# A graph network's adjacency matrix for sorted edges: equal edges summed on VectorE, degrees behind the comparisons, all of it ahead of the branch

## The chip, the core and the metric

The kernel runs on one core of a Trainium2 chip. A core has TensorE (PE in the profile, with weight loads as PEld), VectorE (DVE), ScalarE (ACT), GpSimd (POOL) and SyncE (SP), which run side by side and wait for each other with semaphores. SP and ACT issue the plain DMAs, POOL the indirect ones (scatters and gathers by a list of row numbers). All DMAs share 16 DMA engines. The metric is the device time of one launch in microseconds (us).

## What is computed

A stack of four graph layers over 3125 nodes with 128 features and 50,000 edges, whose list is sorted by destination. Each layer has the form `x = layernorm(x + layer(x))`. The first and the last are chains of graph convolutions (3 and 10 of them); the two between work edge by edge (an attention and a gate). Of these, only what the first needs is touched by the change:

```python
def _gcn_layer(x, src, dst, ew, W, b):
    """PyG GCNConv: out = D^-1/2 (A + I) D^-1/2 (x W) + b."""
    n = x.shape[0]
    loop = jnp.arange(n)
    s = jnp.concatenate([src, loop])
    d = jnp.concatenate([dst, loop])
    w = jnp.concatenate([ew, jnp.ones((n,), ew.dtype)])
    deg = jax.ops.segment_sum(w, d, num_segments=n)
    dinv = jnp.where(deg > 0, jax.lax.rsqrt(deg), 0.0)
    norm = dinv[s] * w * dinv[d]
    h = x @ W
    out = jax.ops.segment_sum(h[s] * norm[:, None], d, num_segments=n)
    return out + b
```

## The kernel before

**The adjacency matrix.** A convolution is done as a dense product: the kernel writes A + I, 3200 x 3125 in float32, into DRAM, and each of the 13 convolutions streams it through PE (line 625, tile `acc`). The matrix lies in seven banks of 464 columns, numbered 0 to 6, in two DRAM tables: `adj0` (banks 0 to 3) and `adj4` (banks 4 to 6); the profile calls both `adj`. A convolution takes the banks from 6 down to 0, 50 matmuls each, in chunks that SP loads (`adj_k`; some chunks stay in SBUF). `Convolutions` also multiplies by the weights (`po`) one bank later.

**Filling it.** `fill` (105) makes a tile `eye` on POOL (a memset of 6320 elements and a copy of the identity) and has ACT issue one DMA of 5.8 MB per bank that writes the identity. Then the edges are added by POOL: 406 indirect scatters (517), each with 128 single values `total` to 128 addresses `at`. A scatter writes, it doesn't add. So edges with equal source and destination must first be summed into the first of them, and the later ones sent to spare rows ahead of the matrix.

**Sorted and unsorted edges.** `stretches` (221) loads the destinations as one run of 392 per partition (`run`: 127 rows in one DMA and the last row in another), tests that they are sorted and spread as expected, and leaves a flag. Every engine reads the flag and branches (1509 to 1511). The branch for sorted edges is the one that runs here; the other one builds the matrix by a general method (`build`, 270).

**Preparing sorted edges.** `SortedBuild` cuts the 28 stretches of 14 x 128 edges into five overlapping passes; each knows which banks its edges can fall into (first and last stretch, first and last bank, and the bank from which the banks are complete after it):

```python
PASSES = ((20, 28, 4, 7, 5), (16, 20, 4, 5, 4), (12, 17, 0, 4, 3), (3, 12, 0, 3, 1), (0, 3, 0, 1, 0))
```

Pass q is loaded as three windows (`src_w`, `dst_w`, `ew_w`) with C = 112, 56, 70, 126 or 42 edges per partition and W = 39 neighbours to the left, to the right or both. Where a window would reach past either end of the list (passes 0 and 4) it is loaded as 127 rows and one row. The method `prepare` (400) has an inner function of the same name (416). For a pass that does, all in order on DVE: a `key` per edge; `same`, 39 comparisons with the neighbours; `more`, the weights of the equal ones. PE then adds these up in `sum`: 39 float32 matmuls with the identity for the weights of later equal edges (two passes of PE each in the profile) and 39 bfloat16 ones to see whether an equal edge came before. DVE goes on with some 20 small operations on C elements (addresses, `lo` and `hi` of the destination). `degrees` (478) handles 14 columns of edges: DVE makes the one-hot tiles `ohl` (14 x 128) and `ohh` (14 x 25, times the weight), and 14 float32 matmuls add them into `deg_ps`. `settle` (463) reads `sum` and forms `total` and `at`. The order is written out by hand with `InOrder`: for each pass prepare, four groups of degrees, settle; then the rest of the 28 groups of degrees. Last come `deg`, a square root on ACT, and `dinv` (508). A pass's scatters are issued when the first convolution comes to a bank that needs them (510 to 525); that bank's loads wait for the pass's last eight scatters.

**Order around it.** `fill` for banks 6 to 4, the test, and the windows of pass 0 are ahead of the branch (1505 to 1508); `load_edges` (138) loads `dst_i`, `src_i`, `ew_c` and the features `x` on SP's and ACT's queues. Behind the branch are a second `eye` with the fills of banks 3 to 0, the other passes' windows, the five passes and the degrees, and then the first layer `l0` with its three convolutions. Its operands are `xs = x * dinv`, so it begins behind `dinv`. SP, ACT and POOL each work their instructions off in order. A DMA from SP or ACT reuses one of eight semaphores in turn, and waits until the earlier DMA on it has landed.

Of the kernel before, what the change touches and what calls it, by code (L numbers as in the profile page):

```python
# [9 lines left out]
F32 = mybir.dt.float32  # L10
I32 = mybir.dt.int32
# [37 lines left out]
def tile_gnn_stack(ctx: ExitStack, tc: tile.TileContext, a: dict, out: bass.AP):  # L49
# [55 lines left out]
    def fill(pool, banks):  # L105
        wide = NP - P + NBK * BW
        eye = pool.tile([P, wide], F32, name="eye")
        nc.gpsimd.memset(eye, 0.0)
        nc.gpsimd.tensor_copy(eye[:, NP - P:NP], ident)
        for b in banks:  # L110
            v = eye[:, b * BW:b * BW + BW]
            nc.scalar.dma_start(bank(b), bass.AP(tensor=v.tensor, offset=v.offset,
                                                 ap=[v.ap[0], [P, NT], [1, BW]]))
# [24 lines left out]
    def load_edges():  # L138
        nc.sync.dma_start(dst_i, a["dst_c"])
        nc.scalar.dma_start(src_i, a["src_c"])  # L140
        nc.sync.dma_start(ew_c, a["ew_c"])
        nc.vector.tensor_copy(dst_f, dst_i)
        nc.scalar.dma_start(x, a["x"].rearrange("(t p) d -> p t d", p=P))
# [126 lines left out]
    def build():  # L270
        with (
# [9 lines left out]
            fill(b1, reversed(range(HALF)))  # L281
# [81 lines left out]
    class SortedBuild:  # L363
# [5 lines left out]
        def __init__(self, early):  # L369
            self.at, self.total, self.ready, self.last = [], [], {}, []  # L370
            self.passes = list(enumerate(PASSES))
            self.st = [self.load(early, 0)]
# [27 lines left out]
        def prepare(self, pool, scratch, ps):  # L400
# [5 lines left out]
            ident_b = scratch.tile([P, P], BF16, name="ident_b")  # L406
            ve.tensor_copy(ident_b, ident)
            deg_ps = ps.tile([P, NT], F32, name="deg_ps")
# [7 lines left out]
            def prepare(q):  # L416
# [4 lines left out]
                both = ps.tile([P, 512], F32, name="both")  # L421
                ve.tensor_copy(both[:, :W + C], key[:, :W + C])
                ve.tensor_copy(both[:, 256:256 + C + W], t["ew"])
                same = scratch.tile([P, W, W + CM], BF16, name="same")[:, :, :W + C]
                ve.tensor_tensor(same, shifts(key, 1, W + C),
                                 both[:, None, :W + C].to_broadcast([P, W, W + C]), op=OP.is_equal)
                more = scratch.tile([P, W, CM], F32, name="more")[:, :, :C]
                ve.tensor_tensor(more, same[:, :, W:], shifts(both, 257, C), op=OP.mult)
                t["sum"] = ps.tile([P, 2, 256], F32, name="sum")
                for k in range(W):  # L430
                    pe_.matmul(t["sum"][:, 0, :C], ident, more[:, k, :], start=(k == 0), stop=(k == W - 1))
                for k in range(W):
                    pe_.matmul(t["sum"][:, 1, :C], ident_b, same[:, k, W - 1 - k:W - 1 - k + C],
                               start=(k == 0), stop=(k == W - 1))

                t["own"] = own = scratch.tile([P, C], F32, name=f"own{q}")
                ve.tensor_tensor(own, t["src"][:, mid], t["dst"][:, mid], op=OP.is_equal)
                ve.tensor_add(own, own, t["ew"][:, :C])
                dst = scratch.tile([P, C], F32, name=f"dst_f{q}")
                ve.tensor_copy(dst, t["dst"][:, mid])  # L440
                t["at"] = scratch.tile([P, C], F32, name=f"at_f{q}")
                t["outer"] = scratch.tile([P, C], F32, name=f"outer{q}")
# [3 lines left out]
                adj_index(ve, t["at"], hi_i, step, t["src"][:, mid], dst, int(lo >= HALF), lo, hi, t["outer"])  # L446

                t["inner"] = inner = scratch.tile([P, C], F32, name=f"inner{q}")
                ve.scalar_tensor_tensor(inner, t["outer"], 0.5, t["ew"][:, :C], op0=OP.is_lt, op1=OP.mult)
                spare = scratch.tile([P, C], I32, name=f"spare{q}")  # L450
                nc.gpsimd.iota(spare, pattern=[[1, C]], base=t["e0"], channel_multiplier=C)
                t["away"] = away = scratch.tile([P, C], F32, name=f"away{q}")
                ve.tensor_tensor(away, spare, t["at"], op=OP.subtract)
# [9 lines left out]
            def settle(q):  # L463
                t = st[q]
                C = t["C"]
                total = pool.tile([P, C], F32, name=f"total{q}")
                ve.tensor_add(total, t["own"], t["sum"][:, 0, :C])
                ve.tensor_max(t["outer"], t["outer"], t["sum"][:, 1, :C])
                ve.scalar_tensor_tensor(t["away"], t["outer"], 0.5, t["away"], op0=OP.is_gt, op1=OP.mult)
                at = pool.tile([P, C], I32, name=f"at{q}")  # L470
                ve.tensor_add(at, t["away"], t["at"])
                self.total.append(total)
                self.at.append(at)

            groups = [(q, g) for q, (s0, s1, _, _, _) in enumerate(PASSES) for g in range(s1 - s0)]
            n_groups = len(groups)

            def degrees(n):
                q, g = groups[n]
                t, c = st[q], slice(g * SC, g * SC + SC)  # L480
                ohl = scratch.tile([P, SC, P], F32, name="ohl", bufs=2)
                ve.tensor_tensor(ohl, iota_ps[:, None, :].to_broadcast([P, SC, P]),
                                 t["lo"][:, c, None].to_broadcast([P, SC, P]), op=OP.is_equal)
                ohh = scratch.tile([P, SC, NT], F32, name="ohh", bufs=2)
                ve.tensor_tensor(ohh, iota_ps[:, None, :NT].to_broadcast([P, SC, NT]),
                                 t["hi"][:, c, None].to_broadcast([P, SC, NT]), op=OP.is_equal)
                ve.tensor_mul(ohh, ohh, t["inner"][:, c, None].to_broadcast([P, SC, NT]))
                for i in range(SC):
                    pe_.matmul(deg_ps, ohl[:, i, :], ohh[:, i, :], start=(n == 0 and i == 0),
                               stop=(n == n_groups - 1 and i == SC - 1))  # L490


            n = 0
            for q in range(len(PASSES)):
                prepare(q)
                while groups[n][0] <= q and n < 4 * q + 4:
                    degrees(n)
                    n += 1
                settle(q)
            for n in range(n, n_groups):  # L500
                degrees(n)
            deg = scratch.tile([P, NT], F32, name="deg")
            ve.tensor_scalar_add(deg, deg_ps, 1.0)
# [1001 lines left out]
    with tc.tile_pool(name="eye", bufs=1, side="right") as pool:  # L1505
        fill(pool, reversed(range(HALF, NBK)))
        flag = stretches()
        built = SortedBuild(early)
    flag = nc.values_load(flag, min_val=0, max_val=1)
    load_edges()  # L1510
    with tc.If(flag == 1) as sorted_edges:
        with tc.tile_pool(name="sb", bufs=1) as one:
            with (
                tc.tile_pool(name="sb_scratch", bufs=1) as scratch,
                tc.tile_pool(name="sb_ps", bufs=1, space=PSUM) as ps,
            ):
                fill(scratch, reversed(range(HALF)))
                built.prepare(one, scratch, ps)
            l0(built)
        l1_sorted()  # L1520
        l2_sorted()
        l3()
    with sorted_edges.Else():
        writers.clear()
        build()
        l0()
        l1()
        l2()
        l3()
# [34 lines left out]
```

## Time and profile before

| | us |
|---|---|
| timed, median of 3 (range) | 3537.91 (3535.11 to 3540.27) |
| the profiled execution | 4306.1 |
| its span, first to last instruction | 4304.4 |
| front: to the first matmul of a convolution | 771 |
| the three convolutions of the first layer | 771 to 1184 |
| second layer: first to last gather on POOL | 1252 to 1931 |
| third layer: first to last gather on POOL | 2096 to 2833 |
| the ten convolutions of the last layer | 2946 to the end |

| engine | busy, us | share of the span |
|---|---|---|
| PE | 3111.9 | 72% |
| DVE | 1552.8 | 36% |
| POOL | 1146.3 | 27% |
| ACT | 789.4 | 18% |

A page of the profile gives such shares, the span in 40 slices, the chain of work that ended last, and groups of instructions as `line engine operation out<-in, shape, count | busy, mean ns of one | idle time before them and what ended most of it`. Line 169 is the helper `InOrder`, through which many instructions are issued, so those are told apart by their tiles. A view by time gives the start and duration of each instruction in us; "issue" as a releaser means that the engine waited for nothing that the profile shows. PE's clock can be throttled; the granted share of full speed is shown by slice (0.5 over most of the front, 1.0 in the convolutions).

### The profile page before, as it was taken

The page shows a single profiled execution, that of the slowest core. Times are in us where ns is not written, and L with a number is a line of the kernel's source. Part 1 is how long each engine was busy: PE and PEld are TensorE (multiplying, and loading weights), DVE is VectorE, ACT ScalarE, POOL GpSimd, SP SyncE. Part 2 cuts the span into 40 slices and gives each one's busy share as a digit, 9 for nine tenths or more (in the row PEclk, how much of TensorE's full clock was granted, in tenths as well). Part 3 has the DMA queues.
Part 4 walks back from the last instruction along what each step waited for, and adds up shares of the span by engine and source line. Part 5 has one row for each costly group of instructions (what it writes and reads, how often), then busy time and mean ns, then how long its engine had stood idle before and what let it go on. Part 6 is the DMA issues. An engine that isn't in the chain of part 4 may idle for free.

```text
span 4304.4 us, 35045 instructions
## 1 busy us (share of the span) xinstructions
PE 3111.9 (72%) x12342; PEld 2052.3 (48%) x12370; DVE 1552.8 (36%) x4377; ACT 789.4 (18%) x1249; POOL 1146.3 (27%) x1207
## 2 busy tenths in 40 slices
PE   4044306999943566666466666659999999999998
PEld 4033306555532555655155555545555555555554
DVE  5022103101231455546256666665222222322234
ACT  0000000000020011111344444442121211111112
POOL 2755563000024555550344444410000000000000
PEclk8555555899955777777688888889999999999999
DMA  8310000766632333223444444448666666666665
GB/s 312 111 36 1 1 0 1 256 224 209 209 104 53 73 75 76 75 72 72 153 126 131 131 130 130 127 116 280 205 220 218 212 204 209 219 219 206 208 207 191
DMA packets 442341, 624.10 MB, mean 145 GB/s; under 512 B 89991, under 2 KB 410171, under 8 KB 442139
## 3 DMA queue, kind: packets, MB, share of 16 engines
q1 hardware_dynamic: 362378, 498.27, 36.2%
q0 software_dynamic: 44352, 77.35, 6.7%
q10 hardware_dynamic: 35424, 46.15, 3.1%
q8 instruction: 99, 1.62, 0.1%
q14 instruction: 88, 0.71, 0.1%
HBM read 557.45 MB, written 64.38 MB: 144 GB/s over the span
## 4 chain that ended last, share of the span: by engine, by line
PE 59%; issue 11%; DVE 5%; DMA 2%; another core or an unknown queue 1%; ACT 1%; POOL 1%; SPq 0%; DVEq 0%; POOLq 0%; ACTq 0%
PE acc L625 39%; PE sums L169 6%; PE pz L169 6%; PE zT L169 4%; PE pe L169 2%; PE po L637 2%; POOL xj L197 1%; DVE z L169 1%; ACT parts L924 1%; DMA x<-s_after 1%; DVE of_edge L169 1%; DVE msg L169 0%; DVE pz L169 0%; DVE h L926 0%
## 5 line engine op out<-in xcount | busy, mean ns | idle before, releaser
L625 PE MATMUL acc<-adj_k,xs 128*128 128x464 f32 (+1 forms) x3280 | 1262.1, 540 | 0.0
L625 PEld LDWEIGHTS acc<-adj_k,xs 128*128 128x128 f32 x3280 | 619.0, 190 | 593.4 <-issue 557.6
L197 POOL DMA_INDIRECT xj<-s_right,src_o x392 | 373.0, 952 | 841.6 <-ACT parts L924 534.8
L197 POOL DMA_INDIRECT zj<-s_to_src,src_i x392 | 370.7, 946 | 531.6 <-DVE z L169 256.0
L625 PE MATMUL acc<-adj,xs 128*128 128x464 f32 (+1 forms) x1270 | 493.1, 534 | 8.1 <-issue 8.1
L517 POOL DMA_INDIRECT adj<-total,at x406 | 389.6, 960 | 297.6 <-DVE key L169 140.9
L169 PE MATMUL sums<-msg,of_edge 128*128 128x132 f32 (+1 forms) x1568 | 285.5, 333 | 191.1 <-issue 174.8
L169 PEld LDWEIGHTS sums<-msg,of_edge 128*128 128x128 f32 x1568 | 253.0, 240 | 215.5 <-issue 198.6
L625 PEld LDWEIGHTS acc<-adj,xs 128*128 128x128 f32 x1270 | 240.0, 191 | 220.9 <-issue 196.9
L169 PE MATMUL pz<-w,eaT 128*128 128x256 f32 x784 | 267.3, 426 | 84.1 <-DVE msg L169 44.3
L169 PE MATMUL sum<-more,ident 128*128 128x112 f32 (+4 forms) x390 | 86.6, 352 | 292.2 <-issue 246.1
L647 DVE SCALAR_TENSOR_TENSOR v<-po,dinv,three 128x128 f32<-128x128 f32 x250 | 71.1, 344 | 589.2 <-PE po L637 589.2
L169 PE MATMUL zT<-ident,xj 128*128 128x128 f32 x784 | 160.1, 331 | 145.2 <-issue 137.3
L169 DVE TENSOR_TENSOR ohl<-iota_b,lo_f 128x1792 f32<-128x1792 f32 x29 | 58.7, 2023 | 545.6 <-PE deg_ps L169 500.3
L169 DVE TENSOR_TENSOR z<-pz,zj 128x1024 f32<-128x1024 f32 (+1 forms) x112 | 122.0, 1089 | 310.8 <-remote 262.2
L169 PEld LDWEIGHTS zT<-ident,xj 128*128 128x128 f32 x784 | 143.1, 240 | 174.1 <-issue 158.6
L169 PEld LDWEIGHTS sum<-more,ident 128*128 128x128 f32 x390 | 85.2, 290 | 290.1 <-issue 284.2
L169 PE MATMUL pz<-td,of_node 128*128 128x256 bf16 x1176 | 209.8, 291 | 14.0 <-DVE z L169 10.2
L169 PE MATMUL deg_ps<-ohh,ohl 128*128 128x25 f32 x812 | 164.8, 370 | 35.7 <-issue 26.2
L169 PE MATMUL pe<-att,leaky 128*128 128x4 f32 x784 | 117.9, 263 | 96.8 <-issue 92.2
L169 PEld LDWEIGHTS pz<-w,eaT 128*128 128x128 f32 x784 | 134.3, 214 | 107.0 <-DVE msg L169 52.8
L169 DVE TENSOR_TENSOR leaky<-zT,leaky 128x512 f32<-128x512 f32 (+1 forms) x112 | 69.2, 619 | 318.7 <-ACT leaky L169 181.7
(183 smaller groups left out, 3166.0 us busy)
## 6 DMA issues: line engine op xcount, KB each, us to landing
adj_k<-adj SPq DMA_DIRECT2D x289, 1160.0 KB
adj<-eye ACTq DMA_DIRECT2D x7, 5800.0 KB
adj_k<-adj SPq DMA_DIRECT2D x39, 852.5 KB
adj<-adj SPq DMA_DIRECT2D x15, 1160.0 KB
eaT<-in_ea_t SPq DMA_DIRECT2D x56, 256.0 KB
drow<-s_local SPq DMA_DIRECT2D x28, 448.0 KB
eaT<-in_ea_t SPq DMA_DIRECT2D x56, 192.0 KB
drow<-s_local SPq DMA_DIRECT2D x56, 128.0 KB
```

The source lines that it names most:

```text
L169: ins = getattr(self.engine, name)(*args, **kwargs)
L197: after_writers(nc.gpsimd.indirect_dma_start(out=to, out_offset=None, in_=table[:NP, :], in_offset=bass.IndirectOffsetOnAxis(ap=index[:, c ...
L517: s = nc.gpsimd.indirect_dma_start(out=table[:SPARE + (hi - b0) * NP * BW, :], out_offset=bass.IndirectOffsetOnAxis(ap=self.at[q][:, c:c + ...
L625: nc.tensor.matmul(acc[:, :c1 - c0], xs[:, t, :], k[:, n % CK, :c1 - c0], start=(n == 0), stop=(n == NT - 1))
L637: nc.tensor.matmul(po[:, t - t0, :], self.aggT[:, t * P:(t + 1) * P], w, start=True, stop=True)
L647: nc.vector.scalar_tensor_tensor(to[:, t - t0, :], sums[:, t - t0, :], dinv[:, t:t + 1], bias, op0=OP.mult, op1=OP.add)
L924: last = nc.scalar.activation(to[:, i], of, AF.Copy)
```

## The change

The constructor of `SortedBuild`, the test, all seven fills and all of `prepare` now stand ahead of the branch, with their tiles in a pool that is released there. The windows of all passes are loaded there too. Behind the branch `load_nodes` loads `x`, `src_i` and `dst_i` on SP; `ew_c` is loaded in the other branch only. There is one `eye` instead of two.

The inner `prepare` and `settle` become `compare`: the sums come from two `tensor_reduce` on DVE, over strided views of `more` and `same`, and `total` and `at` are formed at once. `compare` runs for all five passes first. Then come the degrees: `split` cuts the weight into three bfloat16 parts that add up to it, `ohl` and `ohh` are bfloat16, `ohw` holds `ohh` times each of the three parts (14 x 3 x 25), and 14 bfloat16 matmuls of 75 columns add them into `deg_ps`, which a reduce over the three parts then sums. The number of scatters, their order and the convolutions stay.

```diff
-    def load_edges():
+    def load_nodes():
+        nc.sync.dma_start(x, a["x"].rearrange("(t p) d -> p t d", p=P))
+        nc.sync.dma_start(src_i, a["src_c"])
         nc.sync.dma_start(dst_i, a["dst_c"])
-        nc.scalar.dma_start(src_i, a["src_c"])
-        nc.sync.dma_start(ew_c, a["ew_c"])
         nc.vector.tensor_copy(dst_f, dst_i)
-        nc.scalar.dma_start(x, a["x"].rearrange("(t p) d -> p t d", p=P))
...
-            def prepare(q):
+            def compare(q):
...
-                both = ps.tile([P, 512], F32, name="both")
+                both = ps.tile([P, 512], F32, name="both", bufs=2)
...
-                t["sum"] = ps.tile([P, 2, 256], F32, name="sum")
-                for k in range(W):
-                    pe_.matmul(t["sum"][:, 0, :C], ident, more[:, k, :], start=(k == 0), stop=(k == W - 1))
-                for k in range(W):
-                    pe_.matmul(t["sum"][:, 1, :C], ident_b, same[:, k, W - 1 - k:W - 1 - k + C],
-                               start=(k == 0), stop=(k == W - 1))
+                rest = scratch.tile([P, C], F32, name=f"rest{q}")
+                ve.tensor_reduce(rest, more[:, :, :C].rearrange("p k c -> p c k"), axis=AX.X, op=OP.add)
+
+                before = scratch.tile([P, C], F32, name=f"before{q}")
+                v = same[:, 0, W - 1:W - 1 + C]
+                ve.tensor_reduce(before, bass.AP(tensor=v.tensor, offset=v.offset,
+                                                 ap=[v.ap[0], [1, C], [W + CM - 1, W]]),
+                                 axis=AX.X, op=OP.max)
...
+            def split(q):
...
+                t["inner"] = three = scratch.tile([P, C, 3], BF16, name=f"three{q}")
+                for i in range(3):
+                    ve.tensor_copy(three[:, :, i], inner)
+                    if i < 2:
+                        ve.tensor_sub(inner, inner, three[:, :, i])
...
-                ve.tensor_mul(ohh, ohh, t["inner"][:, c, None].to_broadcast([P, SC, NT]))
+                ohw = scratch.tile([P, SC, 3, NT], BF16, name="ohw", bufs=2)
+                ve.tensor_tensor(ohw, ohh[:, :, None, :].to_broadcast([P, SC, 3, NT]),
+                                 t["inner"][:, c, :, None].to_broadcast([P, SC, 3, NT]), op=OP.mult)
                 for i in range(SC):
-                    pe_.matmul(deg_ps, ohl[:, i, :], ohh[:, i, :], start=(n == 0 and i == 0),
-                               stop=(n == n_groups - 1 and i == SC - 1))
-
-
-            n = 0
+                    pe_.matmul(deg_ps, ohl[:, i, :], ohw[:, i], start=(first and i == 0),
+                               stop=(last and i == SC - 1))
+
             for q in range(len(PASSES)):
-                prepare(q)
-                while groups[n][0] <= q and n < 4 * q + 4:
-                    degrees(n)
-                    n += 1
-                settle(q)
-            for n in range(n, n_groups):
-                degrees(n)
+                compare(q)
+            groups = [(q, g) for q, (s0, s1, _, _, _) in enumerate(PASSES) for g in range(s1 - s0)]
+            for n, (q, g) in enumerate(groups):
+                if g == 0:
+                    split(q)
+                degrees(q, g, n == 0, n == len(groups) - 1)
...
-    with tc.tile_pool(name="eye", bufs=1, side="right") as pool:
-        fill(pool, reversed(range(HALF, NBK)))
+    with (
+        tc.tile_pool(name="front", bufs=1, side="right") as scratch,
+        tc.tile_pool(name="front_ps", bufs=1, space=PSUM) as ps,
+    ):
+        built = SortedBuild(scratch)
         flag = stretches()
-        built = SortedBuild(early)
+        fill(scratch, reversed(range(NBK)))
+        built.prepare(early, scratch, ps)
     flag = nc.values_load(flag, min_val=0, max_val=1)
-    load_edges()
     with tc.If(flag == 1) as sorted_edges:
-        with tc.tile_pool(name="sb", bufs=1) as one:
...
-                fill(scratch, reversed(range(HALF)))
-                built.prepare(one, scratch, ps)
-            l0(built)
+        load_nodes()
+        l0(built)
```

## Prediction

> **What bounds the kernel now.** I began with the page. Its span is not the time to be predicted:
>
> ```profile
> span 4304.4 us, 35045 instructions
> ```
>
> The execution took 4306.1 us, 1.7 around the span; the timed runs have a median of 3537.9, so the profiled execution is 768 us longer. Which of its waits are in the timed runs has to be settled first. In the timeline of the front, PE stands between its matmuls for no shown reason while POOL scatters:
>
> ```profile
> 550.92 0.23 PE L169 MATMUL sum<-more,ident 128*128 128x42 f32 x1 [2.57 <-issue]
> 551.23 0.96 POOL L517 DMA_INDIRECT adj<-total,at  x1 [0.30 <-issue]
> ```
>
> The bracket is PE's idle time before the matmul: one every 2.8 us, against 0.14 us (11.05 us for 78) before POOL had begun. The same gaps lie in both edge layers: the chain of waits puts "issue" at 31.6% of 1170 to 2035 us and 23.9% of 2035 to 2930, or 487 us. Are they in the timed runs? POOL's gathers give a budget, read from the view of the tiles xj and zj (duration min/median/max, first and last start):
>
> ```profile
> L197 POOL DMA_INDIRECT xj<-s_right,src_o x392: 938/944/1347, 1252.1 to 1931.0; - x196
> ```
> ```profile
> L197 POOL DMA_INDIRECT zj<-s_to_src,src_i x392: 940/946/977, 2095.8 to 2833.2; - x196
> ```
>
> 392 gathers at 1.25 us (0.95 and a gap of 0.30) need 490 us and took 679 and 737, so at this pace these layers can be at most 189 + 247 = 436 us shorter. The convolutions run at granted clock 1.0 and leave nothing. The missing 332 us must come out of the front. What could the front give? Its row:
>
> ```profile
> L517 POOL DMA_INDIRECT adj<-total,at x406 | 389.6, 960 | 297.6 <-DVE key L169 140.9
> L169 DVE TENSOR_TENSOR ohl<-iota_b,lo_f 128x1792 f32<-128x1792 f32 x29 | 58.7, 2023 | 545.6 <-PE deg_ps L169 500.3
> ```
>
> The 406 scatters step at 1.26 us (112 took from 87.0 to 228.5), 513 us in all; between passes POOL stood 118 us more for indices from DVE, which waited for stalled PE. Begun at 87.0 without these gaps they end at 600; the first convolution, which needs the last bank (17 us of loading at 350 GB/s, some 8 us of matmuls behind it), ends near 625 and not at 914 as profiled: 289 us. 436 + 289 = 725 of 768; 37 ns less for each of 1190 POOL steps would close the rest. So I take the timed front as **bound by POOL's 406 scatters**, with PE's gaps belonging to profiling. The degrees aren't late there: without gaps `dinv` comes near 345 us (an estimate: 87, then 24 groups at 5.97, four passes of sums at 20 to 32, 20 of DVE), and four banks at 20 us are done by 425, before pass 3's columns are written at 547.
>
> Then the question is when the first scatter starts. Now it ends this chain (start, duration, engine, line, operation):
>
> ```profile
> 51.18 6.29 DVE L169 TENSOR_TENSOR same<-key,both 128x5889 bf16<-128x5889 f32 x1
> 57.51 4.70 DVE L169 TENSOR_TENSOR more<-same,both 128x4368 f32<-128x4368 bf16 x1
> ...
> 62.58 11.05 PE L169 MATMUL sum<-more,ident 128*128 128x112 f32 x78 [40.45 <-DVE own L169]
> ...
> 73.47 2.10 PE L169 MATMUL sum<-same,ident_b 128*128 128x112 bf16 x39
> 75.41 19.23 PE L169 MATMUL deg_ps<-ohh,ohl 128*128 128x25 f32 x112
> ...
> 86.45 0.27 DVE L169 TENSOR_TENSOR at<-away,at_f 128x112 int32<-128x112 f32 x1
> ...
> 87.02 1.17 POOL L517 DMA_INDIRECT adj<-total,at  x1 [56.90 <-DVE key L169]
> ...
> 88.50 0.96 POOL L517 DMA_INDIRECT adj<-total,at  x1 [0.30 <-issue]
> ```
>
> `at` waits for sums and four groups of degrees on PE. The high banks' three fills, which the scatter also waits for, had landed near 71 and were not last.
>
> **The change, part by part.**
>
> *Sums.* 78 + 39 matmuls of pass 0 go (62.6 to 75.4), and DVE no longer waits for degrees (to 85.7). In their place come two tensor_reduce over 4368 elements. The nearest row is `more`, 4368 elements in 4.70 us; I take 4.7 each. **A rule against this:** the Trainium skill, "VectorE: DVE Perf Modes", Rules for kernel authors, calls tensor_reduce the slowest DVE operation (one element per cycle) and asks to restructure; at its 0.96 GHz that is 4.6 us, the row's size. "SBUF — State Buffer" (Door 1: The DMA port swizzle) adds that an access which leaves its 16-byte line pays a penalty, and these reads step by 504 and 328 bytes. No row here strides so; I bound a reduce by 4.7 and 9.4 us (twice, an estimate) and take 4.7. By the rule pass 0's indices come 9 us later, which the fills below hide; above 17 us a reduce it would show.
>
> *Loads.* All windows go ahead of the branch, and `x`, `src_i`, `dst_i` behind it, on SP; `ew_c` leaves this branch. Loads of 127 rows use one of 16 DMA engines: while `run` was loading, the view by stretches has (last two columns: DMA share, GB/s)
>
> ```profile
> 12.00:14.00 2.00, 0.00 (x0) 0.00 (x0) 0.00 (x0) 0.00 (x0) 0.00 (x0) 1.00 0.07 23
> ...
> 32.00:34.00 2.00, 0.00 (x0) 0.00 (x0) 0.00 (x0) 0.00 (x0) 0.00 (x0) 1.00 1.05 384
> ```
>
> 0.07 is one engine, at 24 GB/s; beside fills such a load took 10 to 13 us. In the changed kernel's order of instructions pass 0's three windows and then `run` are at the head: 96.5 + 96.5 + 77 + 219 KB = 489 KB, or 20.4 us at 24 GB/s. From 2.3, with 2 us to land, `run` is there at 24.5 instead of 19.4, pass 0's windows before it (50.8 now, behind `x` and the fills).
>
> *Pass 0 in DVE.* The flag's operations on `run` stand in front: 5 us, to 29.5. `same` 6.3, `more` 4.7, two reduces 9.4, 18 small operations at 0.24: `at` at about 54.5, against 86.5. The flag itself waits behind `same` (36 us); POOL, which queues its scatters behind the flag, needs `at` anyway.
>
> *Fills.* All seven come from one `eye`, ahead of the branch, so a memset of 5.4 us leaves POOL, off its path. But ACT's first fill now waits for the semaphore that `src_w` of pass 3, the sixteenth load, gives back, and the next two for that pass's other windows. That load sits behind `run` on the shared engine: about 26 us. Data starts 1.2 later; three fills took 20.6 to 71 and take 27 to 77.5, landed at **79**. That is later than 54.5: the fills are what is late next.
>
> *Scatters.* First at 79 instead of 87.0, then 406 steps as before; later passes' indices follow each 14 to 28 us and are far ahead. **Second rule:** the Trainium skill, "SBUF — State Buffer", Who interferes with whom, says that a DVE copy in a two-port mode locks GpSimd out, so that its DMA descriptors starve. 15 copies into three parts and pass 0's four casts now fall beside the scatters: 19 x 0.2 = 4 us if each held POOL up in full. The trace has DVE busy from 87 to 103, with POOL at 1.26 a step but for one of 1.48 us, and 1.26 when DVE stood still (190 to 220). I take nothing.
>
> *Degrees.* On DVE per group: `ohl` 2.02, `ohh` 0.51, `ohw` 1050 elements at 1.05 ns and 0.14 (the line through those two) 1.24 us; 28 x 3.77 = 106, splits 11. Comparing ends near 128 (`same` 25, `more` 17, reduces 35, small ones 22, from 29.5), `dinv` comes near 250. PE's 14 bf16 matmuls per group (0.054 us each in the row of `sum<-same`) hide under it. The slack to 459 (pass 3's end 539, less 80) covers doubled reduces (+35). SP's `src_i` load now waits for the last fill, near 142, and holds the adjacency loads behind it: they are not wanted before 250. PE, DVE and ACT come to the branch only behind the degrees; behind it they have what needs `dinv`.
>
> Sum: 79 - 87 = **-8 us**; the chain behind the scatters is untouched. 3538 - 8 = 3530. In the profiled execution the sum is another: 784 PE instructions of the degrees meet the scatters at 1.4 us each, some 340 issue before the scatters end at 592, `dinv` comes near 655 and the first convolution ends at 800 for 914: a span near 4190.
>
> **The rivals.**
> *PE's gaps are real.* Then the 114 us of the last sum are gained: 3424; a part of them, something between. For: no cause is shown for the gaps. Against: the budget, which would need POOL at (1416 - 768) / 784 = 0.83 us a gather, with nothing else late in those layers.
> *The fills start too late (slower).* If the four single-engine loads take the 10 us each that they took beside other traffic, `src_w` of pass 3 lands near 44, the fills at 96, the first scatter 9 us later than now: 3547. It decides from 37 us on. For it: these loads now stand ahead of every fill. Against: nothing else moves then, `x` is gone.
> *Hidden anyway.* Were both starts bound by the same fills, or the end by something behind the scatters, nothing moves: 3538. Against: in the trace fills ended 16 us before `at`.
>
> **How the numbers follow.** My case 0.75, around -8 with an error of about 9 (place of the fill's start, and what a new layout does to the rest; "hidden anyway" is inside it); gaps real in whole or part 0.12; fills late, or POOL's pace hurt, 0.13. The measurement tells about 0.2%, 7 us, from no change. Of my case 0.40 is beyond that, 0.31 within, 0.04 slower. So faster 0.40 + 0.12 = 0.52, same 0.31, slower 0.17. My case's own range is 3518 to 3545; 3505 to 3552 takes in half of the late fills and the smallest part of real gaps.
>
> **What would show it.** Right: the first scatter at 75 to 85 and last released by a fill, `at` 15 us or more before it; 4.7 us per reduce; no gap between passes; a span shorter by about 100 us where the median hardly moves. Wrong: the median falling by 50 us or more (gaps real); the first scatter after 87; reduces above 17 us; POOL's step above 1.28.

## The result and the profile after

| timed runs, us | median (range) | runs |
|---|---|---|
| the kernel before | 3539.03 (3535.11 to 3541.61) | 7 |
| the changed kernel | 3526.60 (3521.75 to 3529.58) | 7 |

The ratio is 0.9966 (95% interval 0.9954 to 0.9977): 12.4 us less, where 8 were forecast. The time lies in the predicted range; the cause, as the experiments show, is another.

In one of the four sets of runs below, as in the first profile of the kernel before, PE stood idle between its instructions while POOL issued its transfers, and the kernel before took 4300.81 us in 19 timed runs, so each experiment is compared with the kernel before of its own set. The changed kernel was timed only beside the seven runs above: "less than the changed kernel" means the difference of two such gains, each known to 4 or 5 us.

The profile of the changed kernel shows no such gaps, and its execution took 3527.32 us. First the lines that answer to those shown of before: the page's span, the scatters and the degrees' matmuls,

```profile
span 3525.3 us, 33097 instructions
L518 POOL DMA_INDIRECT adj<-total,at x406 | 403.2, 993 | 201.5 <-issue 123.2
L168 PE MATMUL deg_ps<-ohw,ohl 128*128 128x75 bf16 x406 | 30.3, 258 | 214.2 <-DVE ohw L168 214.2
```

the gathers of the two edge layers (view of their tiles),

```profile
L196 POOL DMA_INDIRECT xj<-s_right,src_o x392: 940/944/1290, 985.6 to 1477.8; - x196
```

```profile
L196 POOL DMA_INDIRECT zj<-s_to_src,src_i x392: 940/946/1070, 1602.5 to 2092.3; - x196
```

two stretches of the front (last two columns: DMA share, GB/s),

```profile
12.00:14.00 2.00, 0.00 (x0) 0.00 (x0) 0.00 (x0) 0.00 (x0) 0.00 (x0) 1.00 0.07 22
32.00:34.00 2.00, 0.00 (x0) 0.00 (x0) 2.00 (x1) 0.00 (x0) 0.00 (x0) 1.00 1.04 391
```

and the timeline of pass 0 on DVE and POOL:

```profile
25.84 0.57 DVE L253 SCALAR_TENSOR_TENSOR scr<-run 128x392 f32<-128x392 int32 x1 [7.46 <-DMA run<-in_dst_r]
...
28.93 6.28 DVE L168 TENSOR_TENSOR same<-key,both 128x5889 bf16<-128x5889 f32 x1
...
35.24 4.70 DVE L168 TENSOR_TENSOR more<-same,both 128x4368 f32<-128x4368 bf16 x1
39.98 8.28 DVE L168 TENSOR_REDUCE rest<-more 128x112 f32<-128x4368 f32 x1
48.18 8.36 DVE L168 TENSOR_REDUCE before<-same 128x112 f32<-128x4368 bf16 x1
...
60.74 0.27 DVE L168 TENSOR_TENSOR at<-away,at_f 128x112 int32<-128x112 f32 x1
...
85.97 1.17 POOL L518 DMA_INDIRECT adj<-total,at  x1 [78.03 <-DMA adj<-eye]
```

The gathers take 492 and 490 us at 1.25 us each, as the budget in the prediction had them. One DMA engine works at 22 GB/s while `run` is loading, and all do at 391 with the fills. `run` lands at 25.8, `at` is ready at 61.0, and the first scatter waits another 25 us, released by a fill: that is the predicted order of events. But it starts at 85.97 and not at 79, each `tensor_reduce` takes 8.3 us and not 4.7, and the scatters' row has 403.2 us of work instead of 389.6. By these lines the last scatter (611.65) should be later than before, and the time should not have fallen at all.

### The profile page after: what moved, and what is told of

It reads as the page before. It is cut to its first block, busy times and chain, and to the rows that moved or that the text cites. A ratio compares the mean times of both kernels' runs of the same rounds, so it can differ in the third digit from the quotient of the medians.

```text
span 3525.3 us, 33097 instructions
## 1 busy us (share of the span) xinstructions
PE 2749.9 (78%) x11379; PEld 1728.9 (49%) x11379; DVE 1628.6 (46%) x4412; ACT 795.1 (23%) x1248; POOL 1156.1 (33%) x1205
## 4 chain that ended last, share of the span: by engine, by line
PE 50%; POOL 25%; issue 9%; DMA 7%; DVE 6%; ACT 2%; SPq 1%; ACTq 1%; DVEq 0%; POOLq 0%
PE acc L626 45%; POOL adj L518 11%; POOL xj L196 7%; POOL zj L196 6%; PE po L638 2%; PE sums L168 2%; DMA zj<-s_to_src,src_i 1%; DMA adj<-eye 1%; DMA xj<-s_right,src_o 1%; DVE msg L168 1%; DVE z L168 1%; ACT parts L925 1%; SPq L600 1%; DMA adj<-adj 1%; DMA s_left<-parts 1%
## 5 line engine op out<-in xcount | busy, mean ns | idle before, releaser
L518 POOL DMA_INDIRECT adj<-total,at x406 | 403.2, 993 | 201.5 <-issue 123.2
L168 PE MATMUL pz<-w,eaT 128*128 128x256 f32 x784 | 243.3, 392 | 87.7 <-DVE msg L168 75.6
L168 PE MATMUL sums<-msg,of_edge 128*128 128x132 f32 (+1 forms) x1568 | 235.1, 319 | 15.3 <-DVE msg L168 15.3
L648 DVE SCALAR_TENSOR_TENSOR v<-po,dinv,b 128x128 f32<-128x128 f32 x75 | 21.3, 344 | 475.6 <-PE po L638 475.6
L168 PEld LDWEIGHTS sums<-msg,of_edge 128*128 128x128 f32 x1568 | 228.1, 232 | 16.4 <-DVE msg L168 16.0
L633 ACT ACTIVATE aggT<-acc 128x464 f32<-128x464 f32 (+1 forms) x52 | 27.6, 532 | 790.7 <-PE acc L626 790.7
L168 PE MATMUL deg_ps<-ohw,ohl 128*128 128x75 bf16 x406 | 30.3, 258 | 214.2 <-DVE ohw L168 214.2
L660 ACT ACTIVATE rs<-rs 128x4 f32<-128x4 f32 (+1 forms) x91 | 18.6, 205 | 784.1 <-DVE rs L659 778.5
L631 DVE COPY aggT<-acc 128x464 f32<-128x464 f32 x39 | 25.0, 642 | 293.2 <-PE acc L626 293.2
L168 PEld LDWEIGHTS <-of_node 128*128 128x128 bf16 x1176 | 115.4, 98 | 64.2 <-DVE of_node L168 3.0
L168 ACT ACTIVATE leaky<-zT 128x512 f32<-128x512 f32 (+1 forms) x112 | 60.9, 543 | 373.0 <-PE zT L168 362.1
```

Source lines behind the costliest of these rows:

```text
L168: ins = getattr(self.engine, name)(*args, **kwargs)
L518: s = nc.gpsimd.indirect_dma_start(out=table[:SPARE + (hi - b0) * NP * BW, :], out_offset=bass.IndirectOffsetOnAxis(ap=self.at[q][:, c:c + ...
L631: nc.vector.tensor_copy(self.aggT[:, c0:c1], acc[:, :c1 - c0])
L633: nc.scalar.activation(self.aggT[:, c0:c1], acc[:, :c1 - c0], AF.Copy)
L648: nc.vector.scalar_tensor_tensor(to[:, t - t0, :], sums[:, t - t0, :], dinv[:, t:t + 1], bias, op0=OP.mult, op1=OP.add)
L660: nc.scalar.activation(rs[:, :n], rs[:, :n], AF.Sqrt)
```

## The experiments

### The kernel before once more

No edit; one profile.

> The kernel before, unchanged, for a second profile. Its first profiled execution took 768 us more than the timed ones, with PE idle for no shown reason between its matmuls; the changed kernel's had no such gaps. If those gaps belonged to that one execution, this profile spans about 3536 us. My sum for it without gaps was: first scatter at 87, a step of 1.26 us, last scatter near 600, dinv near 345, first convolution done near 625. From the changed kernel (last scatter 611.7) and the measured 12 us, the last scatter must be near 624 here instead, 24 us later than that sum: theory A says that POOL's step is longer than 1.26 (near 1.32) because a DVE multiply from two SBUF tiles holds scatters up here too; rival B says that POOL still stands between passes for indices (24 us of gaps, step 1.26).

The page and the chain of waits (start, duration, what) around the last scatter:

```profile
span 3536.1 us, 35073 instructions
L517 POOL DMA_INDIRECT adj<-total,at x406 | 390.8, 963 | 180.4 <-issue 123.5
```

```profile
601.27 2.15 DMA adj<-total,at
...
604.16 8.11 DMA adj_k<-adj
612.31 12.16 PE acc L625 x24
...
625.14 19.46 PE acc L625 x50
...
645.49 18.03 PE acc L625 x50
...
664.40 15.77 PE acc L625 x50
```

The first theory falls: this profile has no gaps, scatters begin at 87.9, step by 1.27 us and end at 601.3, just as my sum without gaps had it (600), and `dinv` comes at 314. Both A and B are wrong: scatters are neither slower nor interrupted. The missing time lies behind the last scatter. The group of 15.77 us is mostly bank 6 of the second convolution (341 columns, so shorter); it starts 63 us after the last scatter. The same view of the changed kernel:

```profile
611.65 2.13 DMA adj<-total,at
614.00 5.54 DMA adj<-adj
619.59 8.79 PE acc L626 x14
629.27 18.02 PE acc L626 x50
648.19 15.77 PE acc L626 x50
```

Here it starts 36.5 us after it. Up to it PE did 124 matmuls in the kernel before (24 + 50 + 50) and 64 in the changed one. Why, SP's queue tells, in the kernel before and in the changed one:

```profile
554.38 2.99 SPq L599 DMA_DIRECT2D adj<-adj  x1
557.46 12.01 SPq L599 DMA_DIRECT2D adj_k<-adj  x3
603.70 0.36 SPq L599 DMA_DIRECT2D adj<-adj  x1
```

```profile
568.14 2.86 SPq L600 DMA_DIRECT2D adj<-adj  x1
577.15 12.04 SPq L600 DMA_DIRECT2D adj_k<-adj  x4
614.00 0.36 SPq L600 DMA_DIRECT2D adj<-adj  x1
```

`adj` is a chunk that stays in SBUF, `adj_k` a streamed one. The order on the queue is set when the kernel is built. For the last banks (K kept, k streamed, number the bank):

```
before:   ... K2 k3 k3 k3 K1 k2 k2 k2 K0 k2 k1 k1 k1 k1 k0 k0 k0 k0
changed:  ... K2 k2 k2 k2 k2 K1 k1 k1 k1 k1 K0 k0 k0 k0 k0
```

In the kernel before, K0 stands ahead of bank 2's last chunk and of bank 1's four. K0 waits for the last scatter, so SP stood from 569 to 603.7 with chunks behind it that could have been loaded since pass 3. In the changed kernel they were loaded at 561 to 589, and PE did the rest of bank 2 and all of bank 1 while pass 4 scattered.

From the two profiles, the span splits like this (us; each is a difference of starts shown above, the last row the rest):

| | before | changed | difference |
|---|---|---|---|
| to the first scatter | 87.9 | 86.0 | -1.9 |
| first to last scatter | 513.4 | 525.7 | +12.3 |
| last scatter to bank 6 of the second convolution | 63.1 | 36.5 | -26.6 |
| from there to the end | 2871.7 | 2877.1 | +5.4 |
| span | 3536.1 | 3525.3 | -10.8 |

(Of the last row's 5.4 us, 3.9 lie between the gathers of the two edge layers, where the profiles without PE's gaps differ by up to 5 us with no edit there.)

### SP's order of loads, alone and undone

The kernel before, with a kept chunk behind the streamed ones of the bank before it:

```diff
             if self.built:
                 self.built.after(load, b)
+                if pool is self.one and self.streamed:
+                    follow(load, self.streamed)
+                if pool is self.stream:
+                    self.streamed = load
             return k
```

> The kernel before, with only the order of SP's loads of the matrix in the first convolution changed to that of the changed kernel: a bank's first chunk, which stays in SBUF and needs no buffer but waits for the last scatters of its pass, stands behind the streamed chunks of the bank before it, and no longer ahead of them. Theory: in the kernel before, bank 0's first chunk waits at the head of SP's queue until the last scatter (603.7 us) and holds back bank 1's four chunks and bank 2's last one, which had been complete since pass 3; 60 of PE's matmuls, some 24 us, and about 3 us of loading then fall behind the last scatter. With the new order the time falls by 25 to 29 us to 3509 to 3513 (0.992 to 0.993), the last scatter staying at 601. Then the whole of the measured gain of the change (12 us) is this order, and its own parts cost about 14. Rival: the tail behind the last scatter has another cause (the clock, the place of the kept chunks in SBUF), and the time stays at 3538.

In that set the kernel before took 4300.81 us and this one 4303.15: ratio 1.0002 (0.9993 to 1.0011). The first convolution began at 774 us, behind the last scatter at 719.6, so no order of loads could matter: nothing follows. Again:

> The kernel before with the new order of SP's loads, once more, because in the call before this one the kernel before itself took 4301 us, with PE idle between matmuls as in its first profile, and the first convolution began only at 774 us, behind all scatters: the order of the loads could then not show. If the kernel before takes 3538 here, the theory is as it was: 25 to 29 us less, 3509 to 3513, with the last scatter still near 601; rival: 3538. If it takes 4300 again, both expect no difference.

3517.19 us against 3543.56: 0.9924 (0.9910 to 0.9937), 26.4 us less. The chain of waits has the changed kernel's picture, the scatters ending where they did:

```profile
600.81 2.16 DMA adj<-total,at
...
603.18 5.54 DMA adj<-adj
...
608.76 8.32 PE acc L629 x14
...
617.97 18.03 PE acc L629 x50
...
636.89 15.77 PE acc L629 x50
```

From the last scatter to the group of 15.77 are 36.1 us. The order alone gives twice the gain of the whole change.

The reverse: the changed kernel with K0 loaded ahead of bank 1's streamed chunks (and so for the banks above).

```diff
                         j = n // CK
+                        if self.built and j == 1 and b in (5, 4, 3, 2, 1) and (b - 1, 0) not in self.kept:
+                            self.built.scatter(b - 1)
+                            self.kept[b - 1, 0] = self.load(self.one, f"adj{b - 1}_0", b - 1, 0)
...
+                if pool is self.one:
+                    self.first = load
+                elif self.first:
+                    follow(load, self.first)
```

> The changed kernel with a bank's first, kept chunk loaded ahead of the streamed chunks of the bank before it, nearly as the kernel before has it (there one more chunk, bank 2's last, stands behind bank 0's first). Theory: bank 1's four chunks come behind the last scatter again, 50 matmuls or 20 us and some us of loading: the time rises by 20 to 26 us to 3546 to 3553, 1.0025 to 1.0045 of the kernel before, so that with the old order the change would have been slower. Rival: no change from 3527.

In the set with 4300.81 us: 4257.49, ratio 0.9899 (0.9883 to 0.9914); again nothing on the order, since the convolutions began at 726, behind all scatters (last at 624.8).

> The changed kernel with the old order of SP's loads, once more. If the kernel before takes 3538 to 3544 here: the order's 26 us come back except for bank 2's last chunk, 1.0025 to 1.0045 of the kernel before (some 3549 on a basis of 3540), so that the change's other parts alone are a loss of 10 us or more; rival: 0.9966 as the changed kernel, which would mean that the order decides only in the kernel before. If it takes 4300: 0.990 as in the earlier call, which says nothing on the order.

3544.12 against 3539.53: 1.0013 (1.0006 to 1.0019), slower than before by 4.6 us, and so than the changed kernel by 17.0 (4.6 + 12.4). The direction is as expected and both ratios are on the slow side; the size is below it, and PE's timeline says why:

```profile
599.59 5.22 PE L633 MATMUL acc<-adj_k,xs 128*128 128x464 f32 x13
604.65 4.05 PE L633 MATMUL acc<-adj,xs 128*128 128x464 f32 x10
622.53 3.43 PE L633 MATMUL acc<-adj_k,xs 128*128 128x464 f32 x4 [13.83 <-DMA adj_k<-adj]
```

Bank 1's kept chunk (10 matmuls) and, at 599.6, bank 2's last were done before; only bank 1's other 40 matmuls came behind the last scatter, not the 50 that I had counted, and 60 in the kernel before. The 20 that are missing are another 7.8 us at the 0.39 us of one (19.46 / 50), so that with the full old order the change would have lost some 12 us (an estimate).

### The scatters' step

In the timeline of the changed kernel, degrees and scatters side by side:

```profile
163.19 1.25 DVE L168 TENSOR_TENSOR ohw<-ohh,three 128x1050 bf16<-128x1050 bf16 x1
163.29 1.99 POOL L518 DMA_INDIRECT adj<-total,at  x1 [0.30 <-issue]
...
165.58 0.96 POOL L518 DMA_INDIRECT adj<-total,at  x1 [0.30 <-issue]
```

The scatter that starts inside an `ohw` multiply takes 1.99 us instead of 0.96. There are 15 scatters above 1.5 us, all between 163 and 271, while the 29 `ohw` run (one for each stretch of each pass; two passes share a stretch, so there are 29 groups and not 28). With them the row is 13.4 us longer than 406 times 0.96 (389.8). `ohw` reads two tiles from SBUF. One of them was put into PSUM (its type changed with it):

```diff
-                ohh = scratch.tile([P, SC, NT], BF16, name="ohh", bufs=2)
+                ohh = ps.tile([P, SC, NT], F32, name="ohh", bufs=2)
```

> The changed kernel with ohh as float32 in PSUM instead of bfloat16 in SBUF, so that the multiply ohw reads one tile from SBUF and one from PSUM. Theory: the scatters that took 1.97 us instead of 0.96 during an ohw multiply were held up because that multiply reads two tiles from SBUF; now all take about 0.96 and POOL's busy time falls from 403 to 390 us, the last scatter from 611.7 to near 599, the time by 11 to 13 us, to about 3514 (0.993 of before). Rival 1: it is the length or the bfloat16 output of the multiply that holds POOL up, whatever its inputs: POOL stays at 403 us and the time at 3527. Rival 2: POOL's time falls but the end doesn't follow, because something else (the low banks' loads) ends last.

3512.00 us against 3537.92: 0.9927 (0.9913 to 0.9940), 25.9 us less than before and 13.5 less than the changed kernel. The same view and the page's row:

```profile
164.31 1.25 DVE L168 TENSOR_TENSOR ohw<-ohh,three 128x1050 bf16<-128x1050 f32 x1
164.60 0.96 POOL L518 DMA_INDIRECT adj<-total,at  x1 [0.30 <-issue]
```

```profile
L518 POOL DMA_INDIRECT adj<-total,at x406 | 389.8, 960 | 201.7 <-issue 122.9
```

The multiply is as long (1.25 us) and writes the same bfloat16 tile; the scatter that starts inside it takes 0.96, and none of the 406 is above 1.43. The last scatter starts at 598.5 instead of 611.7. The theory holds, and rivals 1 and 2 fall; whether the type of `ohh` has a part in it was not tried by itself.

The other way is to undo the degrees: float32 one-hots, `ohh` times the weight in place, float32 matmuls of 25 columns.

```diff
-                ohw = scratch.tile([P, SC, 3, NT], BF16, name="ohw", bufs=2)
-                ve.tensor_tensor(ohw, ohh[:, :, None, :].to_broadcast([P, SC, 3, NT]),
-                                 t["inner"][:, c, :, None].to_broadcast([P, SC, 3, NT]), op=OP.mult)
+                ve.tensor_mul(ohh, ohh, t["inner"][:, c, None].to_broadcast([P, SC, NT]))
```

> The changed kernel with the degrees as before: ohl and ohh in float32, ohh times the weight in place, float32 matmuls of 25 columns; sums, order and loads stay as changed. Theory: the degrees have slack, dinv moves from about 278 to about 330 us without effect, and the multiply that reads two SBUF tiles is 0.52 us instead of 1.25, so POOL loses less: busy 394 to 398 us instead of 403, the time falls by 5 to 9 us, to about 3519 (0.9945 of before): of the whole change the bfloat16 degrees are then a loss. Rival: the degrees' end matters, the first convolutions start late, and the time rises by 10 us or more over the changed kernel.

3511.89 us, 0.9926 (0.9912 to 0.9939): 13.6 us less than the changed kernel, more than the 5 to 9 expected. `dinv` moved from 275 to 334 without effect, as expected. The multiply of two SBUF tiles is still there, but at 0.52 us it catches few scatters: POOL's row is 391.6 us, some 2 above 406 times 0.96, where I had allowed for 4 to 8. So the bfloat16 degrees bring nothing here and cost the 13 us.

### The fills

ACT's first fill waits in the changed kernel until 27.0 for loads of passes 1 to 4. Here those loads are queued behind the first three fills:

```diff
-            nc.scalar.dma_start(bank(b), bass.AP(tensor=v.tensor, offset=v.offset,
+            filled.append(nc.scalar.dma_start(bank(b), bass.AP(tensor=v.tensor, offset=v.offset,
...
-                nc.sync.dma_start(t[p0:p1], bass.AP(tensor=v.tensor, offset=v.offset + e0 + p0 * C - left,
+                ld = nc.sync.dma_start(t[p0:p1], bass.AP(tensor=v.tensor, offset=v.offset + e0 + p0 * C - left,
...
+                if q:
+                    follow(ld, filled[2])
```

> The changed kernel with the windows of passes 1 to 4 loaded behind the first three fills, so that ACT's first fill no longer waits for those loads to land (27.0 us in the changed kernel's profile). Theory: the first scatter is bound by the three high-bank fills; they start near 17 us, behind the memset of eye, and land near 70; the first scatter moves from 86.0 to 70 to 75 and the time falls by 12 to 16 us against the changed kernel: about 3512 us, 0.9925 of the kernel before. Rival 1: the time doesn't move (3527), because the end of the first layer hangs on the low banks' loads or on other traffic, not on the first scatter. Rival 2: the late windows make POOL wait between passes (a gap before pass 1 or 2), and the gain is smaller than 8 us.

3513.82 us, 0.9932 (0.9918 to 0.9945): 11.7 us less than the changed kernel. The first fill is issued at 12.7, the first scatter starts at 72.28, and POOL has no gap between passes. The theory holds, and another chain now ends at nearly the same time:

```profile
36.00 0.57 DVE L255 SCALAR_TENSOR_TENSOR scr<-run 128x392 f32<-128x392 int32 x1 [16.86 <-DMA run<-in_dst_r]
...
70.92 0.27 DVE L170 TENSOR_TENSOR at<-away,at_f 128x112 int32<-128x112 f32 x1
...
72.28 1.17 POOL L522 DMA_INDIRECT adj<-total,at  x1 [64.35 <-DVE both L170]
```

`run`, a load on one DMA engine, lands at 36.0 now that fills run beside it (25.8 in the changed kernel), DVE's comparisons wait for it, and `at` ends at 71.2. But the profile's releaser (`both`, of pass 1) is not what the first scatter needs. The third fill still is: SP's next load, which waits for that fill, goes at 71.42, and the scatter starts 0.9 us later, as in the changed kernel (landed at 85.0, started at 85.97). So the fills bind here too, with `at` only 0.2 us ahead of them.

### Both together, and the flag behind pass 0

Both edits, first in the set in which the kernel before took 4300.81 us:

> The changed kernel with both edits that helped it: windows of passes 1 to 4 behind the first fills, and ohh in PSUM. Theory: they act on different terms of the same sum (the first scatter 14 us earlier, the scatters' step 13 us less in all) and add: 3526.6 - 12.8 - 14.6 = 3499 (0.989). Rival: with earlier scatters the degrees or the low banks' fills become late and the gain is less than 20 us.

4246.51, 0.9873 (0.9858 to 0.9888); `dinv` at 704.9, the degrees' 406 matmuls stretched from 208 to 703. Then:

> The changed kernel with early fills and ohh in PSUM, once more for the same reason. If the kernel before takes 3538 here, the theory is 3499 (0.989), the two gains adding; rival: less than 20 us of gain over the changed kernel, above 3507, because the degrees or the low banks' fills become late. If it takes 4300 again: 4246 as in the call before, 0.987.

3499.99 against 3543.56: 0.9879 (0.9864 to 0.9894), 43.6 us less, with the last scatter at 584.7. The changed kernel's 12.4 and the two gains of 13.5 and 11.7 make 37.6, the lower end of what this interval allows (37.6 to 48.2). In the traces they add more closely: the last scatter is 26.9 us earlier, and 13.2 and 13.1 with one edit each. This version beats both kernels.

The flag's test behind pass 0's comparisons on DVE, ahead of pass 1's, on top of both edits (the first operation that reads `run` follows `at`):

> As the last one, and the test of the sorted flag (which waits for its run of destinations, landing at 36 us beside the fills) stands behind pass 0's comparisons on DVE instead of ahead of them. Theory: in the run with early fills the first scatter at 72.3 was released by DVE, whose comparison began at 39 behind the flag's operations; now it begins near 18, at is there near 51, and the fills, landing near 64 to 68, bind again: first scatter 66 to 70, 3 to 6 us less than the last kernel, 3494 to 3496. Rival: SP, which reads the flag ahead of the other windows, or POOL, which reads it ahead of its scatters, gets it later (near 56) and nothing is gained, or pass 1 is late.

4249.31 in the same set, 0.9878 (0.9862 to 0.9895) beside the 0.9873 without it. The part of the front that it touches lies before POOL's first transfer:

```profile
52.63 0.28 DVE L170 TENSOR_TENSOR at<-away,at_f 128x112 int32<-128x112 f32 x1
...
55.72 0.15 DVE L267 TENSOR_SCALAR yes<-count 128x1 int32<-128x1 f32 x1
...
71.05 0.33 SPq L386 DMA_DIRECT2D dst_w<-in_dst_r  x1
...
71.91 1.17 POOL L525 DMA_INDIRECT adj<-total,at  x1 [63.98 <-DVE more L170]
```

`at` is 17 us earlier (52.6 for 69.9) and the first scatter is not (71.9 for 71.6). The flag is there at 55.9 and SP has read it by 57.1; what remains for POOL to wait for are the three fills. They land near 71 and not at 64 to 68: the load of `dst_w` waits for the third of them (`more`, which the profile names, belongs to pass 1). The expectation took DVE for what released the first scatter of the run with early fills; this run shows that it was the fills there already, so nothing is to be had here.

### What a reduce costs

`more` laid out edge by edge, so that one of the two reduces reads neighbouring values:

```diff
-                more = scratch.tile([P, W, CM], F32, name="more")
+                more = scratch.tile([P, CM, W], F32, name="more")
...
-                ve.tensor_reduce(rest, more[:, :, :C].rearrange("p k c -> p c k"), axis=AX.X, op=OP.add)
+                ve.tensor_reduce(rest, more[:, :C, :], axis=AX.X, op=OP.add)
```

> The changed kernel with more laid out edge by edge, so that the reduce rest reads 39 neighbouring float32 values instead of values 504 bytes apart, and the multiply that makes more writes 156 bytes apart; the reduce before stays strided. Theory: the stride costs, and rest over 4368 elements takes 4.2 to 4.7 us instead of 8.28, while before stays at 8.36. Rival: tensor_reduce itself takes 1.9 ns an element and rest stays at 8.3. In both the time stays near that of the changed kernel (3527 where the kernel before takes 3538), because the fills, not the comparisons, are last before the first scatter; if more takes as long again as it gains, at comes at the same time.

```profile
34.64 8.21 DVE L168 TENSOR_TENSOR more<-same,both 128x4368 f32<-128x4368 bf16 x1
42.89 4.70 DVE L168 TENSOR_REDUCE rest<-more 128x112 f32<-128x4368 f32 x1
47.51 8.36 DVE L168 TENSOR_REDUCE before<-same 128x112 f32<-128x4368 bf16 x1
```

The stride costs, and it costs a write as much as a read: 8.21 us for the multiply that now writes 156 bytes apart (4.70 before), 4.70 for the reduce (8.28 before). 4368 elements are 1.08 ns each when neighbours follow each other and 1.9 when they do not. The sum is the same, `at` comes at 60.1, and the one timed run (3525.24) is where the changed kernel is.

## Why the prediction came out right, step by step

**The bound.** Right for the timed runs: POOL's scatters set the front. My sum for the kernel before without gaps (scatters to 600, `dinv` near 345) is the second profile's 601 and 314. Its end, "the first convolution ... ends near 625", was wrong: bank 0's last 36 matmuls end 14 us after 645.49, near 660. I had priced 17 us of loading and 8 of matmuls for bank 0 alone, and never asked in what order SP loads.

**The chain behind the scatters.** "The chain behind the scatters is untouched" is the step that failed. The diff does not touch the convolutions, but the build set SP's queue differently, which is worth 26 us, twice the whole gain. The first profile could not show it, since there the convolutions began behind all scatters; the order of the instructions on SP's queue, in the two built kernels, could. Why the build chose another order was not tried.

**The start.** The fills as what is late next, and a fill as the first scatter's releaser: right. The gain was 1.9 us, not 8. The term that was off is the end of the fills in the kernel before, taken as 71. There SP's next load waits for the third fill and shows when it has landed (the first profile; the second line is of the view of waits, with us in total, times, longest):

```profile
78.31 0.33 SPq L386 DMA_DIRECT2D dst_w<-in_dst_r  x1
```

```profile
SPq L386 <- DMA adj<-eye: 25.3, 2, 15.4
```

So the three fills took from 20.4 to 78.3, 58 us and not 50.5. In the changed kernel they are as long, from 28.0 to 85.0. With 58 the prediction's own sum has the fills landed at 85 and the first scatter 1 us earlier than before, as it came. Its case against "Hidden anyway", fills that ended 16 us before `at`, was 8 us. In the trace a fill's landing is counted in 16 parts: of the third, 15 come by 71.0 and the last at 78.3. The loads of 127 rows that use one engine beside the fills would explain that (96.5 + 77 KB of pass 0 are 7.2 us at 24 GB/s, an estimate); it was not tried by itself.

**The reduces.** 8.3 us is inside the bounds (4.7 to 9.4), near the upper one; I took the lower. The rule of the Trainium skill, "SBUF — State Buffer" (Door 1), that leaving a 16-byte line costs, was the better guide than the row of `more`, and the last experiment shows it on reads and writes. As predicted it cost nothing, the fills hiding it.

**The scatters' step.** "I take nothing" was wrong by 12 us; the mean step, 1.298 us (525.7 / 405), is above the 1.28 that was named as a sign of error. Of the Trainium skill, "SBUF — State Buffer" (Who interferes with whom), I weighed one rule, for copies, and passed over another: "A DVE instruction with two SBUF inputs contends with a GpSimd instruction that reads SBUF". By the rule 29 multiplies of 1.25 us are in POOL's way; measured, 15 scatters were held up and the row grew by 13.4 us. The same section doubts it for transfers, since making their descriptors needs only the write port ("inferred"); these runs decide for the contention.

**The gaps as profiling.** Wrong. Timed runs show them too, in one set of four, so they do not come from profiling; their cause was not found. That set ran on another chip (number 15) than the other three (12, 3 and 3), and the chip of the first profile is not on record, so whether the condition belongs to one chip or comes and goes stays open. For that condition I had a second sum, `dinv` near 655 and a span near 4190. The changed kernel itself was not run in it; its relatives had `dinv` at 705 to 715 and spans of 4244 to 4254, with ratios of 0.987 to 0.990, so the gain there would be some 1% and not the 2.7% of that sum (4190 / 4304).

So -8 was a sum of one term, of which a quarter came true. The measured -12.4 is made of -1.9, +12.3, -26.6 and what the profiles leave over. That two terms priced at nothing, of +12 and -26, left a total near the forecast is luck. Without the order it would have gone slower, by POOL's pace, which the prediction names and prices at nothing.

## What to carry to other kernels

Compare the order of instructions on every queue, also on those that the diff does not touch: a transfer that waits for the last event of a stage belongs behind all those that can go already. Beside indirect DMAs from POOL, give DVE's two-input operations one input in PSUM, or keep them short. When a profile is a fifth longer than the timed runs, take a second one before pricing anything by it. Read when a transfer has landed from what waits for it.

## What was not expected of the hardware

A DVE multiply of two SBUF tiles (1.25 us) stretched scatters from 0.96 to 1.99 us; with one tile in PSUM it did not. Strides of 156 to 504 bytes cost DVE 1.9 ns an element for 1.08, in reading float32 and bfloat16 and in writing float32. A transfer over all 16 DMA engines (the third fill) had 15 of its 16 parts landed at 71.0 us and the last at 78.3. In one set the kernel before ran at 4301 us (4293 to 4311) as stably as at 3539 in the others, with PE idle between instructions while POOL issued transfers.
